# Moving constant factors to the output side of filtered convolutions, and the first image's filter work, loads and Strassen sums to other places

## The chip, the cores and the metric

One core of one Trainium2 chip. The time is device microseconds of one execution; several executions give a median. The profiler takes one execution apart by engine: PE is TensorE, PEld its weight loads, DVE is VectorE, ACT is ScalarE, POOL is GpSimd, SP is SyncE (which here only issues transfers). Ratios are the mean time of one kernel's fast runs over that of the kernel before in the same rounds, so they are not quite the ratio of the medians. Stage lengths come from the one profiled run of each kernel.

## The reference, cut to what matters

Eight images of 512 channels of 32 x 32 go through group norm, a 1x1 convolution (cv1), two bottlenecks with a 3x3 convolution and an attention of four heads each, and a last 1x1 convolution (cv2) over all parts.

```python
t = cbs(x, cv1_w, cv1_bn, 0)                     # 1x1 convolution, batch norm, silu
ys = [t[:, :C], t[:, C:]]                        # C = 256
for i in range(2):
    yi = ys[-1]
    z = cbs(yi, m_cv1_w[i], m_cv1_bn[i], 1)      # 3x3 convolution
    z = bot_attention(z, m_qkv_w[i], m_rw[i], m_rh[i])
    z = jax.nn.silu(bn_eval(conv2d(z, m_cv2_w[i], 0), m_cv2_bn[i]))
    ys.append(yi + z)
return cbs(jnp.concatenate(ys, axis=1), cv2_w, cv2_bn, 0)
```

## The kernel before: the parts that matter

The 3x3 convolutions are done in a transformed domain (in the manner of Winograd): inputs and filters are transformed, multiplied by TensorE, and transformed back. The filters are transformed once, in image 0, and kept in memory for the later images. For each output block (`oc`) there are three tiles of transformed filters, the "pairs".

```python
def make_u(n, oc, k, us, tag, raw, bufs=1):      # one input block k, all three pairs
    ...
    for i in range(PAIRS):
        if i == 0:
            nc.scalar.mul(other, g1, -4.0)
            tt(both, g0, g2, ALU.add)
            stt(rows[:, 0], both, -4.0, other, ALU.mult, ALU.add)
            stt(rows[:, 1], both, -4.0, other, ALU.mult, ALU.subtract)
        ...
        tt(ends, c0, c2, ALU.add)
        tt(u[:, :, 1, :], ends, c1, ALU.add)
        last = tt(u[:, :, 2, :], ends, c1, ALU.subtract)
        nc.scalar.mul(u[:, :, 0, :], c0, 2.0)
        nc.scalar.mul(u[:, :, 3, :], c2, 2.0)
```

`tt` is VectorE's tensor_tensor, `stt` its scalar_tensor_tensor. cv2 is multiplied by Strassen's scheme: seven operands, three of them quarters of the weights and four of them sums (`make_ws`). Image 0 makes the sums, stores them to memory, and reads all seven operands (`load_ws`), like every later image:

```python
def prepare():                                   # in attention 1 of image 0, at head group 0
    w2 = load_w2()
def ahead():                                     # there at head group 2, in later images at group 1
    if b == 0:
        make_ws(w2)                              # 4 sums on VectorE, then stores of 2 x 1 MB
    three = s.strassen(b, load_ws(), y0, y1)     # 7 loads of 512 KB on SyncE's queue
    for i in range(PAIRS):
        us[0, i] = load_u(0, 0, i)
```

Attention normalises its output by row sums that take four small transfers in a row, all on SyncE's queue: the sums to memory (`s_dram<-s_row`), back in another layout (`sums_all<-s_dram`), their reciprocals to memory (`r_dram<-rc`), and these back as a broadcast (`rs<-r_dram`). Each of the four is called a hop below. Attention works through its heads in groups, numbered from 0. m2 is the 1x1 convolution that closes a bottleneck.

## Time and profile before

| | us |
|---|---|
| time, median of 3 runs (2438.06 to 2441.61) | 2440.2 |
| span of the profiled run | 2438.2 |
| PE busy | 2365.2 |
| PE idle | 73.0 |

The lines are in the prediction. They are best read as a comparison of stages: PE is full from the second image on, so the first image is held against the second, stage by stage.

### The profile page before, as it was taken

How to read it: one execution, taken by the hardware profiler on the slowest of the kernel's cores; microseconds unless marked ns; L12 is line 12 of the kernel's file. 1: busy time of each engine (PE TensorE's matmuls, PEld its weight loads, DVE VectorE, ACT ScalarE, POOL GpSimd, SP SyncE). 2: the span in 40 equal slices, each digit the busy share in tenths (PEclk: the TensorE clock that was granted, in tenths of full speed). 3: DMA queues.
4: the chain of work that ended last, by engine and by line, in shares of the span. 5: the costliest groups of instructions: out<-in, count | busy, mean ns of one | idle time of the engine just before them, and what ended most of it. 6: DMA issues, size and time to landing. Idle time of an engine off the chain costs nothing.

```text
span 2438.2 us, 35434 instructions
## 1 busy us (share of the span) xinstructions
PE 2365.2 (97%) x14514; PEld 1182.4 (48%) x14514; DVE 1593.4 (65%) x2549; ACT 949.2 (39%) x1294; POOL 85.5 (4%) x301
## 2 busy tenths in 40 slices
PE   7789979999999999999999999999999999999998
PEld 4426426454363644636345363644636354363633
DVE  6678547665667657576676666766568665666654
ACT  2353522524326252352524435243342524326252
POOL 1000001000000000000000000100001000000001
PEclk9899989999999999999999999999999999999999
DMA  7122036021060301503034030520216021050202
GB/s 246 65 76 107 15 130 258 11 71 52 27 259 12 116 10 57 225 15 112 15 115 163 15 112 15 191 91 18 105 32 258 11 72 51 28 215 15 70 10 67
DMA packets 90376, 215.19 MB, mean 88 GB/s; under 512 B 27616, under 2 KB 48288, under 8 KB 77664
## 3 DMA queue, kind: packets, MB, share of 16 engines
q1 hardware_dynamic: 76864, 165.11, 19.4%
q0 software_dynamic: 11200, 47.72, 5.1%
q8 instruction: 116, 1.90, 0.3%
q14 instruction: 52, 0.43, 0.1%
q10 hardware_dynamic: 2144, 0.03, 0.0%
HBM read 180.85 MB, written 31.98 MB: 87 GB/s over the span
## 4 chain that ended last, share of the span: by engine, by line
PE 91%; DVE 4%; DMA 1%; ACT 1%; issue 0%; SPq 0%; DVEq 0%; ACTq 0%
PE ps L302 19%; PE av_ps L541 17%; PE l_ps L515 17%; PE c_ps L731 13%; PE c L786 8%; PE c_new L786 6%; PE v_ps L481 5%; PE m_ps L752 5%; PE s_ps L559 1%; PE s_ps L577 1%; DMA rs<-r_dram 1%; DVE acc L527 1%; DMA u<-u 0%; DMA s<-s 0%; DVE v_in L361 0%
## 5 line engine op out<-in xcount | busy, mean ns | idle before, releaser
L519 ACT ACTIVATE pt<-l_ps 128x1024 f32<-128x1024 f32 x512 | 495.0, 1023 | 312.6 <-PE l_ps L515 312.6
L527 DVE TENSOR_TENSOR acc<-acc,pt 128x1024 f32<-128x1024 f32 x384 | 469.6, 1223 | 123.6 <-ACT pt L519 100.0
L541 PE MATMUL av_ps<-pt,vT 64*64 64x512 f32 x4096 | 489.2, 595 | 16.7 <-DVE ao L549 15.2
L515 PE MATMUL l_ps<-q,kr 64*64 64x512 f32 x4096 | 486.9, 593 | 8.5 <-ACT pt L519 8.5
L731 PEld LDWEIGHTS c_ps<-v_in,u 128*128 128x128 f32 x2688 | 302.8, 192 | 12.7 <-issue 6.7
L731 PE MATMUL c_ps<-v_in,u 128*128 128x128 f32 x2688 | 303.8, 275 | 5.2 <-DVE v_in L361 4.0
L541 PEld LDWEIGHTS av_ps<-pt,vT 64*64 64x64 f32 x4096 | 152.7, 134 | 296.6 <-issue 230.3
L515 PEld LDWEIGHTS l_ps<-q,kr 64*64 64x64 f32 x4096 | 153.8, 133 | 289.5 <-issue 267.3
L302 PE MATMUL ps<-x,w 128*128 128x512 f32 x512 | 227.9, 602 | 2.2 <-DVE x L437 2.2
L302 PE MATMUL ps<-z,qkv_sb 128*128 128x512 f32 x512 | 229.2, 595 | 0.4
L525 DVE TENSOR_TENSOR acc<-pt 128x1024 f32<-128x1024 f32 x64 | 78.4, 1225 | 134.9 <-ACT pt L519 134.9
L469 DVE TENSOR_TENSOR kr<-ps,rw_sb 128x512 f32<-128x512 f32 x64 | 41.2, 686 | 186.0 <-PE ps L302 186.0
L302 PEld LDWEIGHTS ps<-x,w 128*128 128x128 f32 x512 | 97.2, 192 | 130.9 <-issue 127.6
L302 PEld LDWEIGHTS ps<-z,qkv_sb 128*128 128x128 f32 x512 | 94.7, 190 | 107.2 <-issue 91.8
L786 PE MATMUL c_new<-t_in,ws 128*128 128x512 f32 x336 | 145.3, 592 | 0.0
L368 ACT COPY m<-c_ps 128x256 f32<-128x256 f32 x96 | 35.4, 369 | 213.4 <-PE c_ps L731 213.4
L481 PE MATMUL v_ps<-qkv_sb,z 128*128 128x256 f32 x512 | 115.7, 379 | 0.0
L752 PE MATMUL m_ps<-ao,m_sb 128*128 128x512 f32 x256 | 112.5, 592 | 0.0
L481 PEld LDWEIGHTS v_ps<-qkv_sb,z 128*128 128x128 f32 x512 | 97.3, 190 | 26.9 <-issue 15.3
L786 PEld LDWEIGHTS c_new<-t_in,ws 128*128 128x128 f32 x336 | 63.8, 190 | 80.4 <-issue 77.0
L615 DVE TENSOR_TENSOR ao<-ao,rs 128x512 f32<-128x512 f32 x64 | 44.1, 689 | 76.4 <-DMA rs<-r_dram 75.9
L288 ACT ACTIVATE m_kept<-m_kept,bh,sh 128x512 f32<-128x512 f32 x42 | 31.9, 806 | 146.0 <-DVE m_kept L869 86.3
(155 smaller groups left out, 2163.3 us busy)
## 6 DMA issues: line engine op xcount, KB each, us to landing
u<-u SPq DMA_DIRECT2D x84, 1024.0 KB
x<-in_x_dram SPq DMA_DIRECT2D x32, 512.0 KB
x_res<-in_x_dram POOLq DMA_DIRECT2D x28, 512.0 KB, 8.9
ws<-s SPq DMA_DIRECT2D x28, 512.0 KB
out_dram<-m_kept POOLq DMA_DIRECT2D x28, 512.0 KB, 7.6
w<-in_cv_w_dram SPq DMA_DIRECT2D x13, 1024.0 KB
u<-u_new POOLq DMA_DIRECT2D x12, 1024.0 KB, 5.2
rs<-r_dram SPq DMA_DIRECT2D x96, 128.0 KB
```

Source lines behind the costliest of these rows:

```text
L302: nc.tensor.matmul(ps[:, half, :], w_of(k), rhs_of(k, half), start=(k == begin), stop=(k == end))
L469: nc.vector.tensor_tensor(dst, img(ps[:, half, :]), rw, ALU.add)
L481: nc.tensor.matmul(ps[:, at, :], z[:, k, ts(j0 + at, P)], qkv_sb[:, n, k, 2 * C : 3 * C], start=(k == 0), stop=(k == NM - 1),)
L515: nc.tensor.matmul(ps[kh * HD : (kh + 1) * HD, hd, :], kr[r, c, o : o + HD], q[r, c, ts(half, HALF)], start=True, stop=True,)
L519: exp = nc.scalar.activation(pt[:, i], ps, AF.Exp, scale=SCALE)
L525: return nc.vector.tensor_tensor(accs[g], pt[:, 0], pt[:, 1], ALU.add)
L527: ins = nc.vector.tensor_tensor(accs[g], accs[g], pt[:, i], ALU.add)
L541: nc.tensor.matmul(avs[g][hd * HD : (hd + 1) * HD, kh, :], vT[r, j, o : o + HD], pt[r, i, hd, :], start=(j == 0), stop=(j == NJ - 1),)
L615: nc.vector.tensor_tensor(dst, dst, rs, ALU.mult)
L731: nc.tensor.matmul(ps[:, row, col, :], us[i][:, k, row, col, :], vs[i][:, k, row, col, :], start=(k == 0), stop=(k == NM - 1),)
L752: nc.tensor.matmul(pss[oc][:, half, :], m2_sb[:, n, k, ts(oc, P)], ao[:, k, ts(half, HALF)], start=(k == 0), stop=(k == NM - 1),)
L786: nc.tensor.matmul(ps[:, o, :], w[:, k, ts(o, P)], rhs[part][:, c, :], start=(k == 0 and not onto), stop=(k == KB - 1), skip_group_check=onto,
```

## The change

Its intent is to take waits out of the first image. The constants of the filters move to places where they cost no operation of their own, so that ScalarE leaves the chain and no scratch tile is needed. Filters are made pair by pair, in the order in which PE uses them; the second convolution's first block is made during the projection rather than inside attention; residual loads leave the start; Strassen's sums come earlier. `tc.issue_after(x)` puts what stands in it behind the instruction x on x's engine. Cut to its core:

```diff
-            nc.scalar.mul(u[:, :, 0, :], c0, 2.0)
-            nc.scalar.mul(u[:, :, 3, :], c2, 2.0)
+        if i == 0:
+            tt(b, g0, g2, ALU.add)
+            tt(a, b, g1, ALU.add)
+            tt(b, b, g1, ALU.subtract)
+        ...
+        tt(minus, u[:, :, 0], u[:, :, 2], ALU.add)
+        tt(plus, minus, plus, ALU.add)
+        return stt(minus, minus, 2.0, plus, ALU.mult, ALU.subtract)
 ... output side
-            nc.vector.tensor_tensor(r[..., 0], ps[:, :, 0, :], r[..., 0], ALU.add)
+            nc.vector.scalar_tensor_tensor(r[..., 0], ps[:, :, 0, :], 2.0, r[..., 0], ALU.mult, ALU.add)
-                tt(ends, ends, sd[:, 0], ALU.add)
+                stt(ends, ends, -6.0, sd[:, 0], ALU.mult, ALU.add)
 ... second block of a convolution, image 0
-                    make_all(n, oc)
+                    with tc.issue_after(last.ins):      # behind the last add of m2, on VectorE
+                        for i in range(PAIRS):
+                            make(n, oc, i)
 ... attention 0
-            if b == 0 and g < NM:
-                make_u(1, 0, g, [us[0, i] for i in range(PAIRS)], "y0", load_raw(1, 0, g, "pt", 3), 2)
+            behind[-1] = lambda: [make(1, 0, i) for i in range(PAIRS)]   # after the projection
 ... attention 1
+        if b == 0:
+            w2 = load_w2()                              # before attention 1
         def prepare():
-            w2 = load_w2()
+            stored = make_ws(w2)                        # head group 0
-        behind = {2: ahead, 0: prepare} if b == 0 else {1: ahead}
+        behind = {1: ahead, ...}                        # loads at head group 1
 ... last stage
+                with tc.issue_after(stored.ins) if stored else nullcontext():
+                    residual()
+                    residual()
```

(Many cuts. The small normalisation loads also go behind x and the weights.)

## The prediction

> **What bounds the kernel now.** I read four views, in this order: the page's totals and 40 slices, a table of stages, TensorE's list of waits, and VectorE's order of work in two of the stages.
>
> The page says that TensorE (PE) is busy for 97% of the span, and its slices are 9 from the seventh on, but for the last.
>
> ```profile
> span 2438.2 us, 35434 instructions
> PE 2365.2 (97%) x14514; PEld 1182.4 (48%) x14514; DVE 1593.4 (65%) x2549; ACT 949.2 (39%) x1294; POOL 85.5 (4%) x301
> PE   7789979999999999999999999999999999999998
> PEclk9899989999999999999999999999999999999999
> ```
>
> So 2438.2 - 2365.2 = 73.0 us are idle, nearly all in the first image and the tail, and in the first slices the clock is lower too. A change that works on the first image can win only there. I cut that image at the boundaries of its stages and put image 1's same stages beside it. Columns: stretch, length, busy time of PE, PEld, DVE, ACT, POOL, granted clock, DMA share, GB/s.
>
> ```profile
> 0.00:18.68 18.68, 1.15 (x4) 1.00 (x4) 7.51 (x19) 1.80 (x2) 4.49 (x23) 1.00 0.94 295
> 18.68:49.32 30.64, 30.64 (x65) 13.39 (x66) 23.26 (x58) 12.36 (x25) 5.18 (x8) 1.00 0.63 214
> 49.32:87.06 37.74, 25.78 (x194) 24.81 (x193) 32.58 (x83) 11.36 (x26) 1.95 (x7) 0.82 0.43 164
> 87.06:180.41 93.35, 83.29 (x605) 32.18 (x604) 65.14 (x101) 48.93 (x71) 2.80 (x6) 0.96 0.16 53
> 216.06:244.35 28.29, 24.69 (x193) 23.94 (x192) 24.97 (x68) 10.47 (x24) 1.82 (x5) 0.88 0.48 187
> 244.35:339.90 95.55, 80.91 (x602) 31.96 (x600) 48.95 (x55) 42.61 (x53) 1.24 (x4) 0.91 0.24 80
> ...
> 419.08:498.35 79.27, 79.24 (x607) 31.95 (x605) 53.05 (x71) 42.61 (x53) 1.20 (x3) 1.00 0.13 47
> ...
> 534.00:555.44 21.44, 21.44 (x194) 21.44 (x192) 17.67 (x48) 4.71 (x9) 0.18 (x2) 1.00 0.76 270
> 555.44:633.75 78.31, 78.28 (x602) 31.55 (x600) 44.37 (x50) 42.62 (x53) 0.17 (x2) 1.00 0.08 24
> ```
>
> The rows of the first group are the head (loads and group norm), cv1, the first 3x3 convolution, attention 0, the second convolution, attention 1; those of the second are attention 0, second convolution and attention 1 of image 1, which I take as undisturbed lengths. The excess of image 0 is 37.74 - 21.44 = 16.3 us, 93.35 - 79.27 = 14.1, 28.29 - 21.44 = 6.9 and 95.55 - 78.31 = 17.2; image 1's first convolution (22.89 us, 396.19 to 419.08) has 1.4 more. Sum 55.9 us. From image 1's second convolution on there is nothing to win until the last image, which the change leaves alone.
>
> The waits say what these stages wait for:
>
> ```profile
> PE av_ps L541 <- DVE ao L549: 14.6, 1, 14.6
> PE gm_ps L410 <- DVE mv L405: 14.5, 1, 14.5
> PE c_ps L731 <- ACT u_new L260: 12.5, 4, 8.3
> PE l_ps L515 <- ACT pt L519: 8.5, 2, 4.3
> PE c_ps L731 <- DVE r_ends L372: 2.3, 1, 2.3
> ```
>
> Line by line: attention 1 waits once, for 14.6 us; the head's first matmul waits for the statistics of x; the convolutions wait for filters still being transformed (u_new); attention 0 waits twice for an exponential. Waits explain less than the excess (in the first convolution 12.0 of 16.3 us): the rest is slow clock after a wait, 0.82 in its row.
>
> **What the Trainium skill says.** "TensorE: Matmul & The Clock Gate", section "What's actually happening": after about 3.4 us of idling the array runs at half rate, and needs about 3.4 us of work to come back. The trace agrees: cv1's first seven weight loads are 0.85 us apart and the later ones 0.43 us, and after the 4.26 us wait in attention 0 eight matmuls took 1.67 us instead of 1.04. So each removed long wait is worth its length plus 1.8 to 3 us.
> "VectorE: DVE Perf Modes", section "The TRN2 errata", gives an fp32 tensor_tensor of N elements (N+151)/0.96 ns. The trace agrees: 0.42 us for 256, 0.55 for 384, 0.69 for 512, 1.22 for 1024. It gives no time for scalar_tensor_tensor; the trace has 416 ns for both forms in the column output (L371 and L372).
> "DMA: Bandwidth & Descriptors", section "Issuing engines are not separate DMA queues": all queues share 16 DMA engines. The trace agrees in the head, with a share of 0.94 while x, residual loads from another queue, filters and weights all move.
>
> **The change, part by part.**
> *Steady state.* Constants move from the filters to the outputs: some tensor_tensor become scalar_tensor_tensor and one the reverse, none is added. Same duration as shown above, VectorE is 65% busy and PE is full: 0 us in images 1 to 7.
>
> *Filter work.* For one output block and one input block VectorE ran 6 operations of 384 elements and 9 of 256 before, and runs the same number after. Start to start they take 0.47 and 0.33 us in the trace, so 6 x 0.47 + 9 x 0.33 = 5.8 us, or up to 7.4 where each waits for the one before it (0.59 and 0.46). What goes is ScalarE's share: before 3 x 0.52 + 6 x 0.41 = 4.0 us in 9 pieces, in the middle of the chain; after one copy of 512 elements, about 0.53 us as the q copies take, with no VectorE input. VectorE's waits for it (4.6 us, 4 times, at L257 in the first 100 us) go. Also the order becomes all of pair 0, then 1, then 2, as PE uses them.
>
> *Head.* Two residual loads of 512 KB issued at 2.7 us, landing by about 10 us, move to attention 1; the small normalisation loads move behind x and w1. Before, the third x tile arrived at 11.39 us. By then some 3.1 MB had moved, x being 2.1. At the measured 295 to 358 GB/s the last x is then there near 9 us, its statistics (1.6 us a tile) end near 11.1 instead of 14.3. Against that stand 1.4 us of filter work put before the normalisation, of which the 1.2 us wait for POOL hides all but 0.2. Gain 3.0; cv1 starts near 15.7.
>
> *First convolution.* VectorE is the limit here. After x is normalised (about 17.8): remaining filters and constants 13.5 us, to 31.3; input transform 15.3 (the stretch 41.5 to 57.3 less one foreign operation), to 46.6; cv1 ends at 15.7 + 30.6 = 46.3, so the first 10.8 us of matmuls run. In that time VectorE needs 2 x 5.8 to 6.3 = about 12.5 for the second block's filters and 7.3 for the first block's outputs, i.e. to 66.4. Pair 0 (5 us, with the outputs of pairs 0 and 1, 3.3) is ready at 55, in time for 57.1. Pair 1 is ready at 64 and wanted at 60.7: a wait of 3.3, plus about 1.5 of slow clock. The excess falls from 16.3 to 4.8: gain 11.5.
>
> *Attention 0.* The filters of the next convolution were made inside attention, with ScalarE pieces in front of its exponentials and a "pt" buffer held. Now 12 to 15 us of VectorE work run during the projection (21 us, of which VectorE has 5.2 of its own). All is done before the third pair of exponentials wants the buffer. Of 14.1 I take 13.
>
> *Second convolution.* Its second block's filters may now begin only after the last add of m2 (206.0). Before, two thirds of the first half were made earlier (187 to 191.8). So some 5 us more of VectorE work fall in here: transform done at +4.7 us from the stage's start, then 12.5 + 7.3, to +24.5; pair 1 at about +22, and 7.2 us of matmuls for pairs 1 and 2, plus slow clock: 30.5 against 28.3. Loss 2.
>
> *Attention 1.* The 14.6 us wait is a queue: at 310.47 SyncE waits to read the Strassen sums that were stored at 303.8 and 305.0; behind five weight loads stands the broadcast of reciprocals (rs), issued at 315.5 and landed at 325.4; VectorE waits for it, and PE for VectorE. Now the sums (4.8 us of VectorE) come two groups earlier and are stored some 14 us before the first read, as in the later images. Of 17.2 I take 16.5. Image 1's wait for u (1.2 us) goes too: 1.
>
> Sum: 3 + 11.5 + 13 - 2 + 16.5 + 1 = 43 us. 2440 - 43 = 2397.
>
> **Rivals.**
> (a) VectorE takes over the whole excess: filters do not get cheaper on it, and the second convolution loses its early start. For: VectorE is busy 32.58 of 37.74 us in the first convolution and 24.97 of 28.29 in the second. Against: four waits for ScalarE disappear, and the order follows PE. It gives back another 10 us: 2407.
> (b) All waits go, since the independent chains of two input blocks are interleaved and the outputs slip behind the filters. For: operations of both kinds are interleaved in the old trace. Then 3 + 55.9, nearly 59 us: 2381.
> (c) The Strassen move gains nothing, as 3.6 MB of weight loads still stand before a broadcast. Against: image 1 has those loads too and loses nothing (78.28 busy of 78.31). It would give 2413.
> (d) The longer output operations slow all images. For nothing: equal durations, and PE at 99.97 of 100 us in mid-run.
>
> **Range and chances.** The head and attention 1 are firm to 2 us each, attention 0 to 4; the two convolutions to 5 each. In eight of ten cases 2387 to 2409 us. Faster by over 2% means below 2391.4, a gain of 49 of the possible 59: chance 0.27. Within 2%: 0.71. Slower: 0.02, for a queue that blocks in a new place.
>
> **What would show it.** cv1's first matmul near 15.7 us; first convolution about 26 us long with one wait near 3 us for VectorE's u_new, none for ScalarE's; attention 0 near 80 us; second convolution 29 to 32; attention 1 near 79; stages from 555 us on unchanged to 0.1 us. A first convolution of 22 us, or a second one under 25, would show my VectorE sums too large; a wait over 4 us in attention 0 for a late filter or buffer would show the moved work landing on the path; a longer stage in mid-run would break the claim of equal operations.

## The result, and the profile after

The changed kernel takes 2406.5 us (median of 4 runs, 2404.68 to 2408.79) against 2440.5 (4 runs, 2438.06 to 2441.61) of the kernel before: ratio 0.9863, interval 0.9845 to 0.9880. The gain is 34 us (1.4%) where 43 were forecast; 2406.5 lies inside the stated range of 2387 to 2409, near its upper end.

The same table of stages for the changed kernel, with the same columns. The rows are image 0's first 3x3 convolution, attention 0, second convolution and attention 1:

```profile
46.02:72.09 26.07, 23.60 (x194) 23.21 (x192) 24.23 (x66) 5.76 (x11) 1.59 (x3) 0.93 0.51 186
72.09:152.24 80.15, 79.24 (x606) 31.94 (x604) 64.16 (x102) 43.65 (x55) 2.80 (x6) 1.00 0.16 60
...
187.90:216.64 28.74, 24.14 (x194) 23.68 (x192) 27.98 (x77) 5.86 (x11) 1.83 (x5) 0.88 0.46 173
216.64:305.97 89.33, 81.27 (x603) 31.94 (x601) 49.15 (x56) 42.71 (x53) 2.69 (x6) 0.94 0.28 101
```

Here every stage ends at the first matmul of the next one. The prediction cut the first convolution of the kernel before at 87.06, where the chain enters the projection; its first projection matmul is at 86.90, so the lengths before become 37.58 and 93.51. With those:

| stage of image 0 | before | after | gain | forecast |
|---|---|---|---|---|
| head | 18.68 | 16.33 | 2.4 | 3.0 |
| cv1 | 30.64 | 29.69 | 1.0 | 0 |
| first convolution | 37.58 | 26.07 | 11.5 | 11.5 |
| attention 0 | 93.51 | 80.15 | 13.4 | 13 |
| second convolution | 28.29 | 28.74 | -0.4 | -2 |
| attention 1 | 95.55 | 89.33 | 6.2 | 16.5 |
| image 1's first convolution | 22.89 | 23.21 | -0.3 | 1 |

The gains add to 33.8 us; the later images are 2.4 us longer (see below), and the two profiled spans differ by 30.9. One stage is off by ten microseconds: attention 1. PE's longest waits in the changed kernel:

```profile
PE gm_ps L411 <- DVE mv L406: 11.4, 1, 11.4
PE s_ps L568 <- DVE acc L536: 4.7, 1, 4.7
PE c_ps L740 <- DVE u_new L256: 4.3, 1, 4.3
...
PE av_ps L550 <- DVE ao L558: 3.7, 3, 2.7
...
PE c_ps L740 <- DVE u_new L260: 1.5, 2, 1.3
```

No line names ScalarE as the releaser of a filter or of an exponential in image 0 any more. The wait of 4.7 us and the 2.7 us among the av_ps waits are new waits in attention 1; the 4.3 us wait stands in the second convolution; the last line is mostly in the first one.

This is attention 1 of image 0 in order of time, from the timeline of the changed kernel. Columns: start, length, engine, what; a bracket says how long the engine had been idle and for what.

```profile
248.38 0.53 POOL L160 DMA_DIRECT2D s<-s  x1 [35.41 <-DVE s L157]
...
254.89 1.04 SPq L148 DMA_DIRECT2D ws<-s  x2
...
258.30 0.89 SPq L148 DMA_DIRECT2D ws<-s  x2
...
259.85 0.56 SPq L575 DMA_DIRECT2D s_dram<-s_row  x1
...
270.59 0.32 SPq L605 DMA_DIRECT2D sums_all<-s_dram  x1
272.11 0.20 DVE L612 RECIPROCAL rc<-sums_all 128x8 f32<-128x8 f32 x1 [9.02 <-DMA sums_all<-s_dram]
...
274.89 1.08 PE L568 MATMUL s_ps<-acc,ones 128*32 128x256 f32 x8 [4.67 <-DVE acc L536]
...
278.71 3.69 PE L550 MATMUL av_ps<-pt,vT 64*64 64x512 f32 x16 [2.74 <-DVE ao L558]
```

Read it from the bottom. PE waits for VectorE; VectorE sits 9.02 us in front of a reciprocal that needs a few kilobytes. The first hop of these was issued at 259.85 and the second could be issued only at 270.59, after 10.7 us. The next group's same hop, issued at 276.43, is through at 278.06, after 1.6 us. In between stand the loads of the Strassen operands. So the stall of the kernel before was not removed, it moved from head group 2 to group 1 and shrank.

The prediction leaned on image 1, which has the same loads and no stall. Its queue in the changed kernel shows why that was no evidence:

```profile
508.42 0.50 SPq L148 DMA_DIRECT2D ws<-s  x1
...
522.28 0.32 SPq L269 DMA_DIRECT2D u<-u  x1
561.96 0.53 SPq L575 DMA_DIRECT2D s_dram<-s_row  x1
```

Image 1's loads go out at 508 to 522 us, some 40 us ahead of its first row sum at 562. Image 0, as it is written here, can't do that: it makes its sums only inside this attention, at 244.6 to 249.3 us.

### The profile page after: what moved, and what is told of

It reads as the page before. It is cut to its first block, busy times and chain, and to the rows that moved or that the text cites. A ratio compares the mean times of both kernels' runs of the same rounds, so it can differ in the third digit from the quotient of the medians.

```text
span 2407.3 us, 35330 instructions
## 1 busy us (share of the span) xinstructions
PE 2358.4 (98%) x14514; PEld 1180.1 (49%) x14514; DVE 1589.4 (66%) x2549; ACT 925.7 (38%) x1230; POOL 85.6 (4%) x301
## 4 chain that ended last, share of the span: by engine, by line
PE 92%; DVE 4%; DMA 3%; ACT 0%; issue 0%; SPq 0%; POOL 0%; ACTq 0%; DVEq 0%
PE ps L303 20%; PE av_ps L550 18%; PE l_ps L524 18%; PE c_ps L740 12%; PE c L795 8%; PE c_new L795 6%; PE m_ps L761 5%; PE v_ps L489 5%; DMA u<-u 1%; PE s_ps L568 1%; PE s_ps L586 1%; DMA rs<-r_dram 0%; DMA s_dram<-s_row 0%; DVE acc L536 0%; DVE v_in L362 0%
```

## The experiments

What is left to explain: why attention 1 kept 10 us of its stall (theory Q: loads that wait for the stored sums block the queue in order; theory T: the bulk in flight on the shared DMA engines delays the small transfers; rival V: VectorE's four sums; rival X: the moved residual loads), which part of the change gained what, and why the second convolution gained nothing. Each run has three timed rounds, with the kernel before on the same chip beside it.

How much one profile can say: four profiles in which nothing of attention 1 was changed in effect (the changed kernel, and the runs "one group later", "inside attention again" and "not held back" below) give it 89.33, 90.00, 89.52 and 88.51 us. A difference of 2 us there is little more than this spread of 1.5, and one of 0.6 is nothing.

### Old places, new arithmetic

```diff
 kernel before
-            nc.scalar.mul(...)  and the old products
+            new filter arithmetic, new output constants; everything else where it was
```

> The kernel before with only the new filter arithmetic and the moved constants; loads, order of the filter work, residual loads and Strassen sums stay where they were before. Theory 1 (most of the two convolution and attention 0 gains come from where the work stands, not from its arithmetic): the first convolution stays above 32 us (before 37.7, after 26.1), attention 0 stays above 86 us (before 93.4, after 80.2), whole time 2425 to 2437. Rival (taking ScalarE out of the chain was the main thing): the first convolution falls below 30 us, attention 0 to 80 to 84 us, whole time 2410 to 2422. Both expect attention 1 at 95 to 96 us and image 1 onwards unchanged, since the output side costs nothing.

Measured 2429.5 us, ratio 0.9955 (0.9938 to 0.9971). The stages, in the order first convolution, attention 0, second convolution, attention 1:

```profile
48.98:78.52 29.54, 24.52 (x193) 24.00 (x192) 25.56 (x70) 5.87 (x11) 1.59 (x3) 0.88 0.48 177
78.52:173.36 94.84, 85.16 (x606) 32.67 (x604) 64.41 (x103) 43.41 (x55) 2.79 (x6) 0.93 0.15 53
209.02:232.39 23.37, 21.95 (x194) 21.59 (x192) 21.41 (x60) 5.88 (x11) 1.25 (x4) 1.00 0.46 158
232.39:329.29 96.90, 80.77 (x602) 31.77 (x600) 51.02 (x61) 42.61 (x53) 1.24 (x4) 0.91 0.24 85
```

Neither theory holds alone. The arithmetic gives the first convolution 8.0 of its 11.5 us (37.6 to 29.5) and the second one 4.9 (28.3 to 23.4). It gives attention 0 nothing (93.5 to 94.8), although ScalarE's pieces are gone but for one copy for each input block: that gain is the place. And the second convolution is 5.4 us shorter here than in the full change, so the moves gave the arithmetic's gain back there. Both theories had expected 95 to 96 us for attention 1; it took 96.90.

### Residual loads at the start again

```diff
-                with tc.issue_after(stored.ins) if stored else nullcontext():
+                with nullcontext():
```

> The changed kernel with the two residual loads of image 0 free to be issued at the start again. Theory: the head loses its gain (cv1's first matmul near 19 us instead of 16.3), and attention 1 of image 0 gets shorter only by what 1 MB of DMA takes, some 2 to 3 us of its 89.3; whole time within 2 us of the changed kernel. Rival (the residual loads are what makes attention 1 stall): attention 1 falls to about 79 to 82 us and the whole time falls by about 5 us.

Measured 2407.3 us, ratio 0.9863. cv1 starts at 18.77 us instead of 16.33, and attention 1 takes 87.19 us instead of 89.33. The head's gain is thus the residual loads' leaving, all of it, and they seem to cost attention 1 2.1 us. Rival X falls as the main cause: without them 87.19 us remain, far above the 79 to 82 that it asked for.

### Strassen loads one group later

```diff
+            behind[2] = behind.pop(1)
```

> The changed kernel with the Strassen weights of image 0 loaded one head group later (group 2), the sums still in group 0. Theory (the stall of attention 1 is a queue: loads that wait for the stored sums stand in SyncE's queue before the row sums and the reciprocals): the sums are long stored when the loads are reached, no load waits for them, attention 1 falls from 89.3 to 79 to 83 us, whole time about 2398. Rival (it is the sheer traffic of 3.6 MB of weights plus u that delays the small transfers): the stall moves to group 2 and stays at 5 us or more, attention 1 above 85 us.

Measured 2407.9 us, ratio 0.9864; attention 1 took 90.00 us. That would favour the rival, but the run tells nothing. SyncE's queue had kept its order:

```profile
255.15 0.86 SPq L148 DMA_DIRECT2D ws<-s  x2
...
258.43 1.03 SPq L148 DMA_DIRECT2D ws<-s  x2
...
260.04 0.55 SPq L575 DMA_DIRECT2D s_dram<-s_row  x1
```

The loads are issued at the same times as before (255.15 and 258.43 against 254.89 and 258.30). The place in the source did not set the place in the queue, for the instructions are issued in another order than the source has them. That also spoils the prediction's "two groups earlier": the sums ran from 244.6, but nothing held the loads back until they were long stored.

### Loads really behind group 0's broadcast

```diff
+            behind[2] = behind.pop(1)
-                    nc.sync.dma_start(rs[...], r_dram[...])
+                    latest[0] = nc.sync.dma_start(rs[...], r_dram[...])
-                three = s.strassen(b, load_ws(), y0, y1)
+                with tc.issue_after(latest[0].ins) if b == 0 else nullcontext():
+                    three = s.strassen(b, load_ws(), y0, y1)     # and the loads of u
```

> The changed kernel with the Strassen weights of image 0 put behind the reciprocals' broadcast of group 0 in SyncE's queue (the run with group 2 had left SyncE's order as it was). The stored sums are then some 15 us old, so no load waits. Theory of the wait in the queue: attention 1 falls to 79 to 82 us. Rival of the traffic: the row sums of group 1 now stand behind 3.6 MB instead of those of group 0, and attention 1 stays above 85 us.

Measured 2403.5 us, ratio 0.9850; attention 1 took 85.91 us. Now no load waits for a sum. Group 0's small transfers are quick, and those of group 1 stand behind the bulk:

```profile
266.91 0.46 SPq L148 DMA_DIRECT2D ws<-in_cv_w_dram  x1
...
271.86 0.53 SPq L577 DMA_DIRECT2D s_dram<-s_row  x1
...
282.35 0.32 SPq L607 DMA_DIRECT2D sums_all<-s_dram  x1
```

The hop takes 10.5 us again. The move was worth 3.4 us of the 10, so attention 1 stays above 85 us, as T says, and far from Q's 79 to 82.

### Row sums from another queue

```diff
+            row_q = nc.gpsimd if at == NM * NH else nc.sync
-                nc.sync.dma_start(s_dram, row[0:P:32, :])
+                row_q.dma_start(s_dram, row[0:P:32, :])          # and the other three hops
```

> The changed kernel with the small transfers of the softmax row sums of image 0's attention 1 issued from GpSimd's queue; weights stay where they are in SyncE's queue, with the same traffic at the same time. Theory of the queue order: the row sums no longer stand behind the loads that wait for the stored sums, attention 1 falls from 89.3 to 79 to 83 us. Rival of the traffic (16 shared DMA engines busy with 3.6 MB of weights): the small transfers still take about 10 us to land and attention 1 stays above 85 us.

Measured 2406.1 us, ratio 0.9856; attention 1 took 88.70 us.

```profile
256.87 0.61 POOL L576 DMA_DIRECT2D s_dram<-s_row  x1 [5.14 <-ACT s_row L575]
263.66 0.58 POOL L606 DMA_DIRECT2D sums_all<-s_dram  x1 [6.18 <-DMA s_dram<-s_row]
270.37 0.20 DVE L613 RECIPROCAL rc<-sums_all 128x8 f32<-128x8 f32 x1 [7.18 <-DMA sums_all<-s_dram]
```

With SyncE's order out of the way, the first hop is issued 3.0 us earlier (256.87 instead of 259.85), but each of the two hops takes 6.7 to 6.8 us and the reciprocal starts only 1.7 us earlier than in the changed kernel. GpSimd's queue is not empty either: the stored sums and the residual loads go out on it from 248.48 us. But the last of these landed by 263.1 us, so nothing of them stood before the second hop, issued at 263.66, and it still took 6.7 us, while in the same run a hop of the same size after the bulk, at 270.88, landed in 1.7. So the main cause is the traffic and not the order of the issuing queue, and theory Q falls as the main cause.

### Plain weights from SBUF, sums still from memory

```diff
+                if b == 0:      # a11, a12, a22 are quarters of tiles that are in SBUF anyway
+                    (a11, _), (a12, a22) = ((w[:, :, :CO], w[:, :, CO:]) for w in w2)
+                    ...         # s1 to s4 loaded from memory as before
```

> The changed kernel in which image 0 takes the three plain Strassen weights from SBUF, but reads the four sums back from memory as now: the loads that wait for the stored sums keep their place in SyncE's queue, 1.5 MB less are moved, about 1 MB of it in the time of the stall. Theory of the wait in the queue: attention 1 stays at 88 to 90 us. Theory of the traffic (1 MB of residual loads was worth 2.1 us): attention 1 falls by 2 to 4 us, to 85 to 87 us.

Measured 2404.9 us, ratio 0.9855; attention 1 took 87.00 us, 2.3 less, at the upper end of T's range (85 to 87) and outside that of Q (88 to 90). The reads of the sums still waited for the stores (the first was issued at 256.35 us), yet the first hop took 8.6 us (258.92 to 267.50) instead of 10.7. Together with the residual loads (1 MB, 2.1 us) there are two doses, of about 1 MB each, that are worth a little over 2 us each; each alone is hardly above the spread of the profiles, so they support T and don't prove it.

### All seven operands from SBUF in image 0

```diff
     def make_ws(w2):
+        kept_sums.extend(sums)
 ...
+                if b == 0:
+                    (a11, _), (a12, a22) = ((w[:, :, :CO], w[:, :, CO:]) for w in w2)
+                    s1, s4, s2, s3 = (w[:, j] for w in kept_sums for j in range(2))
+                    ws = [a11, s1, a12, s4, s2, s3, a22]
+                else:
+                    ws = load_ws()
```

> The changed kernel in which image 0 takes its seven Strassen operands straight from the tiles that are in SBUF anyway (the two weight tiles and the two sum tiles), so that no weight is loaded and no stored sum is waited for in image 0. Theory of the queue, and the rival of the traffic alike: attention 1 of image 0 falls to 78 to 81 us, whole time 2395 to 2399. If instead VectorE's 4.8 us of sums in group 0 are the cause, attention 1 stays above 86 us.

Measured 2396.4 us, ratio 0.9818 (0.9801 to 0.9834); attention 1 took 79.01 us, 0.7 above image 1's 78.31 of the kernel before. VectorE still makes the sums there, and 2 MB of stores and 1 MB of residual loads still go out: rival V falls. A load of filters (u, 1 MB), which stands right behind the operands in the changed kernel, also left this stretch: it goes out at 217 us here and at 259 there. So 3.9 MB less move between 247 and 275 us (3.47 MB against 7.39), and not only the operands are spared. The rate of the DMA engines in 40 slices of 247 to 275 us, first of the changed kernel and then of this one, shows the difference:

```profile
GB/s 0 0 0 114 240 249 424 459 433 410 410 445 351 275 386 339 404 398 334 334 416 396 373 397 405 413 415 416 445 433 319 72 48 0 0 6 0 6 0 0
```

```profile
GB/s 0 386 480 433 316 398 398 269 246 181 357 345 421 240 53 0 5 1 0 12 0 3 3 23 23 143 67 141 0 0 0 0 0 0 6 0 6 0 0 0
```

A slice is 0.7 us. In the changed kernel the bulk ends in slice 31, near 269 us, and the small hop issued at 259.85 is through at 270.59; here it ends in slice 14, near 257 us, and the same hop, issued at 254.79, is through at 257.75.

### Filters made inside attention again

```diff
-            behind[-1] = lambda: [make(1, 0, i) for i in range(PAIRS)]
+                if b == 0:       # in attention 0, head group 0, behind the first sum of exponentials
+                    for i in range(PAIRS):
+                        make(1, 0, i)
```

> The changed kernel with the filters of image 0's second convolution made again inside attention 0 (after the first sums of exponentials of group 0) instead of during the projection; arithmetic as in the changed kernel, no ScalarE piece in the chain. Theory (the place gains attention 0's 13 us, not the arithmetic): attention 0 goes back from 80.2 to 88 to 95 us, whole time about 2416. Rival (ScalarE's pieces in front of the exponentials were the cause): attention 0 stays at 80 to 83 us.

Measured 2418.4 us, ratio 0.9911; attention 0 took 91.60 us instead of 80.15. There an exponential of ScalarE waits 9.6 us for the filter work on VectorE to end, and PE 5.8 us for the exponential. So 11.5 of attention 0's 13.4 us are the place, as the theory said, and the run with old places agrees. Whether VectorE's time or the "pt" buffer that the raw filters hold is what delays the exponential, the runs don't separate.

### Second convolution's filters not held back

```diff
-                    with tc.issue_after(last.ins):
+                    with tc.issue_after(last.ins) if n == 0 else nullcontext():
```

> The changed kernel without the order that holds the second convolution's filters of image 0 back behind the last add of m2. Theory (the new arithmetic gains some 5 us in the second convolution, as the run with old places shows with 23.4 us, and the order gives it back): the second convolution falls from 28.7 to 23 to 25 us, the 4.3 us wait for u_new goes, whole time about 2402. Rival (VectorE has too little free time before, so the work only moves): it stays above 27 us.

Measured 2400.4 us, ratio 0.9836; the second convolution:

```profile
187.85:211.57 23.72, 22.46 (x193) 21.73 (x192) 23.17 (x65) 5.87 (x11) 1.24 (x4) 1.00 0.45 159
```

It is 5.0 us shorter than in the changed kernel, PE's wait of 4.3 us is gone and the clock is 1.00 instead of 0.88. VectorE does 23.17 us of work in it instead of 27.98: the other 4.8 us fit in before the last add of m2 (one block's first operations at 158 to 164.7 us), in time that was free.

### Both together

> Strassen operands of image 0 straight from SBUF together with filters not held back: the two gains stand in different stages and should add. Attention 1 about 79 us, second convolution 23 to 25, whole time 2390 to 2393, faster than both kernels and by over 2% against the kernel before. If they interact (the ring of five weight buffers runs short), the second convolution or image 1's first one gets a new wait over 2 us.

The edit is the two diffs above. Measured 2390.9 us (2388.68 to 2391.48), ratio 0.9793 (0.9776 to 0.9809). The second convolution took 23.71 us and attention 1 79.01, so the gains add. It is faster than both kernels, and 2.07% under the kernel before. "By over 2%", as expected, is not shown: the interval reaches up to 0.9809. No new wait over 2 us appeared.

## Why the prediction was right or wrong, point by point

- **Steady state costs nothing: right.** The operation that adds the row ends was a tensor_tensor before and is a scalar_tensor_tensor after; 692 ns both times, here before and after:

```profile
L395 DVE TENSOR_TENSOR r_ends<-r_ends,sd 128x512 f32<-128x512 f32 x32 | 22.1, 692 | 1.0
```

```profile
L396 DVE SCALAR_TENSOR_TENSOR r_ends<-r_ends,sd 128x512 f32<-128x512 f32 x32 | 22.1, 692 | 1.0
```

  PE is busy for 2005.66 us from image 1's first projection to the end, 2005.15 before. The stretch is 2.4 us longer (2021.56 against 2019.12). About 2 us of that are in the first convolutions of images 2, 4 and 6, where waits of 0.2 to 0.8 us stand, mostly for filters read from memory. The claim "unchanged to 0.1 us" was too narrow. The same stretch runs from 2019.8 to 2023.0 us in the ten experiments, so I don't assign it to the change.
- **Head: right in mechanism, 0.6 us too much.** cv1 starts at 16.33, forecast 15.7; it is the residual loads. Its start varied from 15.22 to 16.66 us between the runs that left the head alone.
- **First convolution: right** in length (26.07, forecast 26) and in what remains (waits for VectorE's u_new). The remainder is two waits of 1.26 and 1.21 us, and not one of 3.3. That the length is met to 0.1 us is luck. Ten profiles have this filter work and these two waits: in five of them, this one included, 3.4 us at half clock follow and the stage takes 26.07 us, in the other five the clock stays at 1.00 and it takes 24.44. (In those, cv1 takes 30.3 to 30.5 us instead of 29.3 to 29.7.) The gain of 1.0 us that the table gives to cv1 is of that kind: its weight loads are 0.85 us apart until 24.8 us before and until 20.7 us after, so 6.1 and 4.4 us at half rate, and no step of the change explains that.
- **Attention 0: right** (80.15, forecast 80), by the place of the work.
- **Second convolution: the mechanism right, the loss too large.** In the profiles that keep the hold it took 28.6 to 29.9 us, a loss of 0.3 to 1.6 where 2 was forecast. The hold behind m2 does cost 5 us, as the sum had it; the new arithmetic was worth 4.9 there, where 5 less the loss of 2 allows it about 3. (A removed long wait was counted as its length plus 1.8 to 3 us; this one, of 4.3 us, was worth 5.0.)
- **Attention 1: the step that failed.** "Now the sums ... come two groups earlier and are stored some 14 us before the first read, as in the later images. Of 17.2 I take 16.5." Measured 6.2. The first read waited for the stores and was issued 6.5 us after the first store (248.38 to 254.89), because nothing tied the loads to their group in the source; with that put right attention 1 fell by 3.4 us. The larger part is that the bulk delays the hops issued while it is in flight, from SyncE's queue and from GpSimd's; without the loads attention 1 fell by 10.3. The prediction called the 14.6 us wait a queue, but its own reading held the sign: rs was issued at 315.5 and landed at 325.4, so two thirds of the wait came after SyncE had issued it. Rival (c) named this cause and was dismissed with image 1, whose loads leave 40 us earlier. The step was called firm to 2 us and was off by 10.
- **Image 1's wait for u: wrong**, 1 us forecast and 0.3 lost; the wait is still there (1.53 us, before 1.22). In the ten experiments this stage took 21.44 to 22.33 us, so the 0.3 are not the change's.

The stages' other errors nearly cancel: apart from attention 1 the table's gains add to 27.6 us, where 26.5 were forecast. So the total stayed in the range with its most certain large term 10 us wrong, because the range left 5 us to each of the two convolutions, which didn't need them.

What stays open: how far the small hop waits behind the bulk of its own queue, and how far among that of the others in the DMA engines. From SyncE's queue it took 10.7 us, from GpSimd's 6.8, with the same bulk going out, though not issued at the same moment.

## What to carry to other kernels

A small transfer that an engine waits for took 10.7 us here beside bulk loads and 1.6 without them, so keep bulk out of the time of such a chain or, better, don't reload what is in SBUF already. When a stall is said to vanish because another stage has the same loads and no stall, check in that stage when the loads were issued. An order edge that is meant to protect one chain can keep work out of free time in another: the hold behind m2 cost as much as the new filter arithmetic had won there.

## What the Trainium skill lacked or had wrong

- "DMA: Bandwidth & Descriptors", "Issuing engines are not separate DMA queues", says that transfers of all engines share 16 DMA engines and interleave. The runs agree, but the page gives no size for what that does to a small one: a row sum hop of 4 KB took 1.6 us in quiet, and 6.8 us from GpSimd's queue and 10.7 us from SyncE's while bulk moved at about 400 GB/s.
- "VectorE: DVE Perf Modes", "The TRN2 errata", gives fp32 tensor_tensor a formula, which held, and doesn't name scalar_tensor_tensor: for both the traces have the same time, 692 ns at 512 elements and 415 to 416 ns at 256 with one operand in PSUM.
- "TensorE: Matmul & The Clock Gate", "What's actually happening", puts the half clock after at least one idle window of about 3.4 us. The second convolution fits that: 0.88 mean clock with its 4.3 us wait, 1.00 without it. The first convolution of the changed kernel doesn't: the clock was 0.50 from 65.0 to 68.4 us, though the waits before it were only 1.26 and 1.21 us long and PE was busy for 1.39 of the 3.4 us before the drop. After the same two waits the run of both edits stayed at 1.00. The section has no case of such short waits.
